# Block sums of turned activations: from VectorE to a GpSimd sequence of their own, with one turning step placed later

## The chip, the cores and the metric

The kernel runs on one core of one Trainium2 chip. The metric is the device time in microseconds (us), lower is better. A core has TensorE (PE in the profile, with its weight loads as PEld), VectorE (DVE), ScalarE (ACT), GpSimd (POOL) and SyncE (SP, which here issues all DMA transfers). Each runs its own instruction stream in order, and waits on semaphores for the others.

## What is computed

Per batch of 8, with 1024 rows of width 1024, in float32:

```
x = x + attention(layernorm(x), ctx, mask)       # 64 memory rows per batch, one head
x = x + base + experts, on h = layernorm(x):
    base    = h @ weight.T                        # 1024 x 1024
    experts = 2.0 * sum over the top 2 of 8 experts of  w_e * (h @ A_e.T) @ B_e.T     # rank 16
```

The dense product `base` takes most of TensorE's time.

## The kernel before, in words

The 8192 rows are 64 tiles of 128 rows; two tiles make a pair (32 pairs), and from pair 2 on four pairs in flight make one turn of the loop `quad(u)` (L973), which finishes the pairs u and v = u+1 and prepares n = u+2, m = u+3 and f = u+4. There are 15 quads, u = 2, 4, ... 30; `first()` (L792) does pairs 0 and 1 and the start-up.

**The dense product is done with block sums** (a Strassen-like scheme). A pair's turned activations form a 2 x 2 grid of blocks: `has[u][:, r]` and `hbs[u][:, r]` are the two halves of the contraction for tile r. `block_sums` (L557) makes four sums of the four blocks, in two steps:

```
s1 = a21 + a22 ; s2 = s1 - a11      # one()
s4 = a12 - s2  ; s3 = a11 - a21     # two()
```

`rt_sums_steps` (L571) calls it for a pair (the pair sums, 128 x 512 each; the names in the profile are `s`), and `joint_sums` (L678) for the two pairs of a quad together (the joint sums, same size; `s_j` and `q_j`). The sums of the weights (`weight_sums`, `quarter_sums`) are made once, in the start-up and the first quad. All of these run on VectorE, by `tt` (`nc.vector.tensor_tensor`). `product(u, i)` (L638) multiplies with the pair sums: product 1 uses `has` itself, 6 uses s2, 7 uses s3; their blocks of 8 matmuls of 128 x 512 are `ch` in the profile.

**The joint products** (`joint`, L692) are where pairs u and v are multiplied together, one quarter of the output columns and rows at a time: joint 5, 3, 2 and 4 in this order at the end of each quad. Each is eight blocks of four (or so) matmuls of 128 x 256. Two PSUM banks are cut into four half banks p2, p5 (names `ju`), p4 and chain (`jl`). What matters here is that p5 and chain are used more than once within a joint product:

```
        block(p5, s1, q1, True)
        part(v, 1, p5)        
        block(chain, s2, q2, False)
        part(u, 1, chain)
        hook(5)
        block(p5, s4, b22, False)
        block(chain, s3, q3, False)
```

(some lines between them are left out; `part` is VectorE's add of a half bank into x, L714). So the block with s4 can start only when VectorE's add of p5 is done. `hook(step)` runs the functions given for that place: it is the way in which work of other stages is written into a joint product.

**Order.** `tc.manual_schedule` (L1125) keeps each listed engine's instructions in the order in which the program writes them; the order is thus written out by hand in `quad`. The lines that matter in a quad: `rt_turn(v)` (L985), pair sums of v (L1017 to L1021), joint sums for joint products 5 and 3 (L1046, L1057), `rt_turn(n)` in hook 5 of joint 3 (L1079), joint sums for 2 and 4 (L1089 to L1091, the second step in hook 2 of joint 2), pair sums of n in hook 5 of joint 4 (L1113).

**Turning.** `rt_turn` (L498) turns the two tiles of a pair: `rt_turn_tile` (L491) issues two VectorE block transposes (STREAM_TRANSPOSE, 128 x 512) from the tile `hs` (loaded by SyncE into `ring`, a pool of 6 buffers) to `has` and `hbs`.

**Buffers.** The pool `sums` has one buffer each for the tags s2, s3, q3 and q4, and two for s14. Pair sums s2 and s3 share the first two with the first and second of the joint sums, so a new sum can be written only after TensorE has read the last one.

Of the kernel before, what the change touches and what calls it, by code (L numbers as in the profile page):

```python
# [14 lines left out]
ALU = mybir.AluOpType  # L15
# [9 lines left out]
def kernel(  # L25
# [10 lines left out]
    nc = tc.nc  # L36
# [37 lines left out]
    mm, tt = nc.tensor.matmul, nc.vector.tensor_tensor  # L74
# [12 lines left out]
    def transpose_blocked(dst, src):  # L87

        nc.vector.transpose(  # L89
            dst.rearrange("p k (t i) -> p t k i", i=NB),  # L90
            src.rearrange("p t (k i) -> p t k i", i=NB),
        )
# [121 lines left out]
    def x_stats(u: int):  # L214
        x_sums(u)
        x_squares(u)
        x_root(u)
# [46 lines left out]
    def f_rows(u: int, fetch: bool = True):  # L264

        nm, std = fts.pop(u)
        rstd = small.tile([P, 2, 1], F32, tag="rstdf", name=f"rstdf_{u}")
        nc.vector.reciprocal(rstd, std)
        nmr = small.tile([P, 2, 1], F32, tag="nmrf", name=f"nmrf_{u}")
        tt(nmr, nm, rstd, ALU.mult)  # L270
        for r in range(2):
            h = ring.tile([P, D], F32, tag="ring", name=f"h_{u}_{r}")
            hss.setdefault(u, []).append(h)
            nc.scalar.activation(  # L274
                h, xts[u][r], AF.Identity, bias=nmr[:, r, :], scale=rstd[:, r, :]
            )
        norm_send(u, fetch)
# [100 lines left out]
    def att_sc(u: int):  # L378
        sc = ps_at.tile([P, 2, M], F32, tag="at", name=f"sc_{u}")
        nc.tensor.transpose(sc.rearrange("p j m -> p (j m)"), scs.pop(u), ident)  # L380
        scs[u] = sc
# [82 lines left out]
    def norm_send(u: int, fetch: bool = True):  # L464

        hds[u] = dram.tile([2 * P, D], F32, tag="hd", name=f"hd_{u}")
        hs_in, hss[u] = hss[u], []
        for r in range(2):
            nc.sync.dma_start(out=hds[u][r * P : (r + 1) * P, :], in_=hs_in[r])
        if fetch:  # L470
            norm_fetch(u)
# [10 lines left out]
    def h_tiles(u: int):  # L482
        has[u] = turned.tile([P, 2, KH, P], F32, tag="hA", name=f"hA_{u}")
        hbs[u] = turned.tile([P, 2, KH, P], F32, tag="hB", name=f"hB_{u}", bufs=3)
# [6 lines left out]
    def rt_turn_tile(u: int, r: int):  # L491
        if r == 0:
            h_tiles(u)
        half = KH * NB
        for t, c in ((has[u], 0), (hbs[u], half)):
            transpose_blocked(t[:, r], hss[u][r][:, :, c : c + half])

    def rt_turn(u: int):  # L498
        for r in range(2):
            rt_turn_tile(u, r)  # L500
# [56 lines left out]
    def block_sums(outs, a11, a12, a21, a22):  # L557

        s1, s2, s3, s4 = outs

        def one():
            tt(s1, a21, a22, ALU.add)
            tt(s2, s1, a11, ALU.subtract)

        def two():
            tt(s4, a12, s2, ALU.subtract)
            tt(s3, a11, a21, ALU.subtract)

        return one, two

# [67 lines left out]
    def product(u: int, i: int, between=None, after: int = 0):  # L638

        if i == 1:  # L640
            pps[u] = bank_of(f"b5_{u}") if u < 2 else None, bank_of(f"ch_{u}")
        b5, chain = pps[u]
        if i == 1:
            block(chain, has[u][:, 0], w11, True, between, after)
        elif i == 5:
            block(b5, sms[u][:, 0], t1, True, between, after)
        elif i == 6:
            block(chain, sss[u][1], t2, False, between, after)
        elif i == 7:
            block(chain, sss[u][2], t3, False, between, after)  # L650
        else:
            lora(u, chain, 1, HB, HB)
# [320 lines left out]
    def quad(u: int):  # L973

        v, n, m, f = [u + i for i in range(1, 5)]
        more = n < NP
        far = f < NP
        b = f // PPB
        new_mem = far and f % PPB == 0

        product(u, 1, (lambda: att_sc(n)) if u == 2 else None, 1)
        pending.pop()()
        product_add(u, 1)
        rt_low_rank_tile(u, 0)
        rt_turn(v)  # L985
        product(u, 6)
        if more:
            x_stats(m)
        if u == 2:
            att_divide(n)  # L990
            att_turn_p(n)
        if more:
            att_turn(m)
        product_add(u, 6)
        if u == 2:
            quarter_sums("t4", t4)
        if new_mem:
            mask_bias(b)
            send_mem(b)
        if far:  # L1000
            load_xs(f)
            load_xt(f)
        rt_low_rank_tile(u, 1)
        product(u, 7)
        rt_top(u)
        product_add(u, 7)
        if more:
            att_readout(n)
            att_scores(m)
            rt_turn_low_rank(u)  # L1010
            att_add(n)

        if more:
            product(v, 1, {0: lambda: att_sc(m), 2: lambda: product(u, 8)})
            att_rstd(m)
            att_exp(m)
            one, two = rt_sums_steps(v)  # L1017
            one()
            product_add(u, 8)
            product_add(v, 1)  # L1020
            two()  # L1021
            f_sums(n)
            att_divide(m)
            rt_low_rank_tile(v, 0)
            product(v, 6, lambda: att_turn_p(m), 1)
            f_squares(n)
        else:
            rt_sums(v)
            product(v, 1, {0: lambda: rt_turn_low_rank(u), 2: lambda: product(u, 8)})
            product_add(u, 8)  # L1030
            product_add(v, 1)
            rt_low_rank_tile(v, 0)
            product(v, 6)
        if far:
            att_turn(f)
        product_add(v, 6)
        rt_low_rank_tile(v, 1)
        product(v, 7)
        if new_mem:
            turn_mem(b)  # L1040
        rt_top(v)
        if more:
            f_std(n)
            f_rows(n)
        product_add(v, 7)
        one, two = joint_sums(5, u)  # L1046
        one()
        if more:
            att_readout(m)
        if far:  # L1050
            att_scores(f)
        if u == 2:
            quarter_sums("w21", w21)
        if more:
            rt_turn_low_rank(v)
            att_add(m)
        two()  # L1057

        def low_v():
            product(v, 8)  # L1060
            product_add(v, 8)

        if more:
            hooks = {2: [low_v]}
        else:
            hooks = {1: [lambda: rt_turn_low_rank(v)], 3: [low_v]}
        if new_mem:
            void_mem(b)
        if far:
            x_sums(f)  # L1070
            x_squares(f)
            x_root(f)
            hooks[3] = [lambda: att_sc(f)]
        end_5 = joint(5, u, hooks)

        hooks = {1: [end_5]}
        if more:
            f_sums(m)
            hooks[5] = [lambda: rt_turn(n)]  # L1079
        if far:  # L1080
            hooks[2] = [lambda: att_rstd(f), lambda: att_exp(f)]
            hooks[7] = [lambda: att_divide(f)]
        end_3 = joint(3, u, hooks)
        if m + 2 < NP:
            load_xs(m + 2)
            if (f + 2) % PPB == 0 and f + 2 < NP:
                load_mem((f + 2) // PPB)

        one, two = joint_sums(2, u)  # L1089
        one()  # L1090
        hooks = {1: [end_3], 2: [two]}  # L1091
        if more:
            f_squares(m)
            f_std(m)
            hooks[1].append(lambda: f_rows(m, False))
        if far:
            hooks[3] = [lambda: att_turn_p(f)]
        end_2 = joint(2, u, hooks)

        def rows_0():  # L1100
            end_2()
            for p in (u, v):
                store(p, 0)
                if not more:
                    store(p, 1, ts(1, HB))
            if more:
                norm_fetch(m)
            if m + 2 < NP:
                load_xt(m + 2)

        hooks = {1: [rows_0]}
        if more:
            hooks[5] = [lambda: rt_sums(n)]  # L1113
        end_4 = joint(4, u, hooks, not more)

        def last():
            end_4()
            if more:
                for p in (u, v):
                    store(p, 1)  # L1120

        pending.append(last)

    engines = mybir.EngineType
    with tc.manual_schedule(engines={engines.PE, engines.DVE, engines.Activation, engines.SP}):  # L1125
        first()
        for q in range(1, NQ):
            quad(2 * q)
        pending.pop()()
# [43 lines left out]
```

## Time and profile before

| | us |
|---|---|
| median of 3 runs (1132.64 to 1134.44) | 1132.66 |
| the profiled execution, whole | 1133.88 |
| its span, first to last instruction | 1132.1 |
| one quad (from 382.38 to 451.20) | 68.82 |
| of it busy: TensorE / VectorE / ScalarE / GpSimd | 68.46 / 51.07 / 34.89 / 0 |
| one block sum on VectorE, 128 x 512 | 0.69 |

The profile is that of one execution. Busy times count instructions that compute; a line such as `L714 DVE TENSOR_TENSOR xt<-ju,xt 128x256` names the line of the kernel, the engine, the operation, and output <- inputs by the program's names with the numbers left out. In a timeline, a line gives the start, the time from the first start to the last end, how many such instructions follow one another, and in brackets idle time of the engine in front of it with what ended it. Matmuls are pipelined and their ends modelled: the distance between the starts of two blocks tells more than the duration of one.

### The profile page before, as it was taken

The numbers are of one execution on the slowest core, as the hardware profiler recorded it, in microseconds if no ns is written. First come the engines' busy times: TensorE is split into PE (matmuls) and PEld (weight loads), VectorE is DVE, ScalarE is ACT, GpSimd is POOL, SyncE is SP. The second block draws the span as 40 slices with busy tenths as digits, with TensorE's granted clock in tenths as the row PEclk, the third lists the DMA queues.
The fourth block names the chain that finished last, engine by engine and source line by source line (L and its number), as shares of the span: only waits on it lengthen the run. The fifth ranks groups of instructions, "written<-read, shape, count | busy, mean of one in ns | idle before, by whom it ended". The sixth has DMA issues, their size and how long they took to land.

```text
span 1132.1 us, 15632 instructions
## 1 busy us (share of the span) xinstructions
PE 1117.1 (99%) x5490; PEld 771.2 (68%) x5490; DVE 850.1 (75%) x2099; ACT 553.8 (49%) x1047; POOL 1.0 (0%) x16
## 2 busy tenths in 40 slices
PE   8999999999999999999999999999999999999998
PEld 5555576775867768676685766758677686766767
DVE  6679887777688677886778767787777877867665
ACT  4576563735537354472635736356373544635010
POOL 0000000000000000000000000000000000000000
PEclk9999999999999999999999999999999999999999
DMA  9966256552664726537263474534645554352401
GB/s 215 234 196 196 75 168 194 161 201 97 173 191 120 234 94 174 169 113 260 89 201 120 150 223 130 186 122 155 189 131 186 153 158 155 112 186 75 150 0 75
DMA packets 104462, 175.73 MB, mean 155 GB/s; under 512 B 11904, under 2 KB 76544, under 8 KB 104384
## 3 DMA queue, kind: packets, MB, share of 16 engines
q1 hardware_dynamic: 104384, 174.73, 50.6%
q8 instruction: 43, 0.70, 0.3%
q14 instruction: 35, 0.29, 0.1%
HBM read 107.84 MB, written 66.85 MB: 154 GB/s over the span
## 4 chain that ended last, share of the span: by engine, by line
PE 81%; DVE 11%; DMA 6%; SPq 1%; issue 1%; DVEq 0%
PE ch L631 28%; PE jl L631 12%; PE pa L513 10%; PE ju L631 9%; PE ro L420 5%; PE sct L367 5%; DVE xt L714 3%; PE ju L623 2%; PE ch L623 2%; PE jl L623 2%; DMA mem<-in_ctx_dram 2%; PE plain L631 2%; DVE hA L89 2%; DVE hB L89 1%; DMA xs<-in_x_dram 1%; SPq L83 1%
## 5 line engine op out<-in xcount | busy, mean ns | idle before, releaser
L631 PE MATMUL ch<-t,s 128*128 128x512 f32 x496 | 224.6, 592 | 0.0
L714 DVE TENSOR_TENSOR xt<-jl,xt 128x256 f32<-128x256 f32 (+1 forms) x301 | 139.2, 484 | 112.7 <-PE jl L631 72.5
L193 ACT ACTIVATE junk<-xt 128x1024 bf16<-128x1024 f32 x60 | 63.3, 1055 | 199.7 <-DMA xt<-in_x_dram 198.3
L631 PEld LDWEIGHTS ch<-t,s 128*128 128x128 f32 x496 | 88.5, 190 | 86.1 <-issue 86.1
L631 PE MATMUL ch<-w,hA 128*128 128x512 f32 x248 | 115.9, 593 | 0.0
L714 DVE TENSOR_TENSOR xt<-ju,xt 128x256 f32<-128x256 f32 (+1 forms) x150 | 80.1, 551 | 42.4 <-PE ju L631 41.5
L620 DVE TENSOR_TENSOR xt<-ch,xt 128x512 f32<-128x512 f32 x124 | 85.0, 685 | 33.9 <-PE ch L631 24.5
L274 ACT ACTIVATE h<-xt,nmrf,rstdf 128x1024 f32<-128x1024 f32 x60 | 71.2, 1234 | 52.5 <-DVE nmrf L270 52.5
L620 DVE TENSOR_TENSOR xt<-ro,xt 128x512 f32<-128x512 f32 x128 | 80.4, 683 | 6.0 <-PE ro L420 6.0
L513 PEld LDWEIGHTS pa<-art_sb,hA 128*128 128x128 f32 x512 | 68.5, 190 | 23.2 <-issue 18.9
L631 PEld LDWEIGHTS ch<-w,hA 128*128 128x128 f32 x248 | 44.7, 190 | 43.0 <-issue 42.1
L89 DVE STREAM_TRANSPOSE xT<-xs 128x1024 f32<-128x1024 f32 x60 | 70.5, 1213 | 0.7 <-DMA xs<-in_x_dram 0.7
L513 PE MATMUL pa<-art_sb,hA 128*128 128x136 f32 x512 | 69.9, 279 | 0.0
L202 ACT ACTIVATE junk<-xt,nm 128x1024 bf16<-128x1024 f32 x60 | 68.9, 1148 | 1.9
L513 PE MATMUL pa<-art_sb,hB 128*128 128x136 f32 x512 | 69.7, 279 | 0.0
L253 ACT ACTIVATE junk<-xt,nmf 128x1024 bf16<-128x1024 f32 x60 | 68.7, 1146 | 1.1
L367 PEld LDWEIGHTS sct<-xT,memT_True 128*64 128x64 f32 x960 | 51.8, 137 | 22.7 <-issue 16.7
L513 PEld LDWEIGHTS pa<-art_sb,hB 128*128 128x128 f32 x512 | 64.1, 190 | 0.0
L420 PE MATMUL ro<-mem,pt 64*128 64x512 f32 x256 | 63.6, 615 | 0.4 <-ACT pt L411 0.4
L243 ACT ACTIVATE junk<-xt 128x1024 bf16<-128x1024 f32 x60 | 62.9, 1049 | 1.6 <-DVE xt L620 0.6
L367 PE MATMUL sct<-xT,memT_True 128*64 128x128 f32 x960 | 59.0, 276 | 0.0
L372 ACT COPY scts<-sct 128x128 f32<-128x128 f32 x32 | 8.5, 266 | 102.5 <-PE sct L367 102.5
(183 smaller groups left out, 1852.1 us busy)
## 6 DMA issues: line engine op xcount, KB each, us to landing
xt<-in_x_dram SPq DMA_DIRECT2D x64, 512.0 KB, 6.2
out_dram<-xt SPq DMA_DIRECT2D x62, 512.0 KB, 3.7
xs<-in_x_dram SPq DMA_DIRECT2D x240, 128.0 KB, 3.8
hd<-h SPq DMA_DIRECT2D x60, 512.0 KB, 2.7
hs<-hd SPq DMA_DIRECT2D x240, 128.0 KB, 3.3
mem<-in_ctx_dram SPq DMA_DIRECT2D x16, 256.0 KB, 5.5
w<-in_w_t_dram SPq DMA_DIRECT2D x16, 256.0 KB, 11.5
md<-memc_False SPq DMA_DIRECT2D x7, 256.0 KB, 2.9
```

What stands on the lines that cost most here:

```text
L89: nc.vector.transpose(dst.rearrange("p k (t i) -> p t k i", i=NB), src.rearrange("p t (k i) -> p t k i", i=NB),)
L193: nc.scalar.activation(nowhere, xts[u][r], AF.Identity, accum_out=sm[:, r, :])
L202: nc.scalar.activation(nowhere, xts[u][r], AF.Square, bias=stds[u][:, r, :], accum_out=ss[:, r, :],)
L253: nc.scalar.activation(nowhere, xts[u][r], AF.Square, bias=nm[:, r, :], accum_out=ss[:, r, :])
L274: nc.scalar.activation(h, xts[u][r], AF.Identity, bias=nmr[:, r, :], scale=rstd[:, r, :])
L367: mm(sct[r * M : (r + 1) * M, :], mt[:, k, :], x_ts[u][r][:, k, :], start=(k == 0), stop=(k == KD - 1),)
L420: mm(ro, pts[u][rows, :], m[rows, ts(c, HB)], start=True, stop=True)
L513: mm(pa[:, r, :], h, art_sb[:, k, :], start=(k == 0), stop=(k == KD - 1))
L620: tt(xc, bank, xc, ALU.add)
L623: mm(bank, axwts[u][:, r, :], lb_sb[:, c0 : c0 + n], start=alone, stop=True, skip_group_check=True)
L631: mm(bank, a[:, k, :], w[:, k, :], start=(start and k == 0), stop=(k == n - 1), skip_group_check=True)
L714: tt(xc, src, xc, ALU.add)
```

## The change

The four operations of `block_sums` are issued on GpSimd instead of VectorE, for pair sums and joint sums alike, in the start-up too. GpSimd is added to the engines whose order is that of the program, so its sums form one sequence in the written order. In `quad`, the turning of pair n is divided: tile 0 stays in hook 5 of joint 3, tile 1 goes to hook 5 of joint 2.

```diff
         s1, s2, s3, s4 = outs
 
+        by = nc.gpsimd.tensor_tensor
+
         def one():
-            tt(s1, a21, a22, ALU.add)
-            tt(s2, s1, a11, ALU.subtract)
+            by(s1, a21, a22, ALU.add)
+            by(s2, s1, a11, ALU.subtract)
 
         def two():
-            tt(s4, a12, s2, ALU.subtract)
-            tt(s3, a11, a21, ALU.subtract)
+            by(s4, a12, s2, ALU.subtract)
+            by(s3, a11, a21, ALU.subtract)
...
             f_sums(m)
-            hooks[5] = [lambda: rt_turn(n)]
+            hooks[5] = [lambda: rt_turn_tile(n, 0)]
...
             hooks[1].append(lambda: f_rows(m, False))
+            hooks[5] = [lambda: rt_turn_tile(n, 1)]
...
-    with tc.manual_schedule(engines={engines.PE, engines.DVE, engines.Activation, engines.SP}):
+    with tc.manual_schedule(engines={engines.PE, engines.DVE, engines.Activation, engines.SP, engines.Pool}):
```

## The prediction

> **What bounds the kernel now.** I read the page's busy times first, then the windows of several repetitions of the loop over groups of four pairs (a "quad", 15 of them), then TensorE's waits, then the timelines of TensorE and VectorE inside one quad.
>
> ```profile
> PE 1117.1 (99%) x5490; PEld 771.2 (68%) x5490; DVE 850.1 (75%) x2099; ACT 553.8 (49%) x1047; POOL 1.0 (0%) x16
> ```
>
> ```profile
> 313.56:382.38 68.82, 68.46 (x341) 48.01 (x341) 53.89 (x135) 35.93 (x67) 0.00 (x0) 1.00 0.51 160
> 382.38:451.20 68.82, 68.46 (x342) 48.02 (x341) 51.07 (x127) 34.89 (x66) 0.00 (x0) 1.00 0.53 162
> ```
>
> Columns of the second view: length of the window, then busy time (and instructions) of PE, PEld, DVE, ACT, POOL, then granted clock, DMA share, GB/s. A quad takes 68.82 us and TensorE is busy in all but 0.36 of it, at full clock. A matmul's recorded end is modelled, so I look at starts: a block of four 128x256 matmuls follows the last one after 0.86 us nearly everywhere, and one place breaks the pitch.
>
> ```profile
> 430.83 1.03 PE L631 MATMUL ju<-w,s_j 128*128 128x256 f32 x4
> 431.70 1.03 PE L631 MATMUL jl<-w,s_j 128*128 128x256 f32 x4
> 432.56 1.03 PE L631 MATMUL ju<-w,q_j 128*128 128x256 f32 x4
> ...
> 438.75 1.03 PE L631 MATMUL ju<-w,s_j 128*128 128x256 f32 x4
> 439.62 1.03 PE L631 MATMUL jl<-w,s_j 128*128 128x256 f32 x4
> 441.01 1.13 PE L631 MATMUL ju<-w,q_j 128*128 128x256 f32 x4 [0.36 <-DVE xt L714]
> ```
>
> These are the same three steps (s1 into p5, s2 into the chain, s4 into p5 again) of joint 3 (430.83) and of joint 2 (438.75). Joint 3 keeps the pitch. In joint 2 the third step should start at 439.62+0.86 = 440.48 and starts at 441.01: 0.53 us late. The reason is on VectorE, which must empty p5 before TensorE may write it again:
>
> ```profile
> 431.90 0.42 DVE L714 TENSOR_TENSOR xt<-ju,xt 128x256 f32<-128x256 f32 x1
> ...
> 439.33 0.68 DVE L566 TENSOR_TENSOR q_j<-hB,s_j 128x512 f32<-128x512 f32 x1
> 439.93 0.69 DVE L567 TENSOR_TENSOR q_j<-hB,hB 128x512 f32<-128x512 f32 x1
> 440.53 0.42 DVE L714 TENSOR_TENSOR xt<-ju,xt 128x256 f32<-128x256 f32 x1
> ```
>
> In joint 3 that add starts 0.20 after its block's pitch ends (431.70 to 431.90). In joint 2 it could start at 439.8, but stands behind two block sums and starts at 440.53. The view of TensorE's waits has this as the only one of size:
>
> ```profile
> PE ju L631 <- DVE xt L714: 4.7, 13, 0.4
> ```
>
> Thirteen times, once in each quad up to the one at 933 us. The kernel is bound by TensorE's instruction stream; VectorE costs time only there.
>
> **What the change can gain.** 13 x 0.53 = 6.9 us. In the quad at 1002 us the same step is 0.24 late (1058.17 where 1057.93 is due): +0.2. In the first quad, joint 5 starts its s2 step at 149.00 where 148.54 is due and its s4 step at 150.26 where 149.86 is due, with block sums at 147.00 to 148.20 in front of the adds on VectorE. Other quads lose 0.15 in joint 5 (425.55 for 425.40), where two adds stand between the steps and no sum does; that stays. So the first quad has 0.46+0.40-0.15 = 0.7 to give. Sum: 6.9+0.2+0.7 = 7.8 us. More cannot come of it: the rest of the stream stands at its pitch, apart from 15 x 0.15 = 2.2 us in joint 5.
>
> **What is taken from VectorE.** 124 instructions of the pair sums and 120 of the joint sums:
>
> ```profile
> L563 DVE TENSOR_TENSOR s<-s,hA 128x512 f32<-128x512 f32 x31 | 21.4, 691 | 1.1
> L566 DVE TENSOR_TENSOR s<-hB,s 128x512 f32<-128x512 f32 x31 | 21.3, 687 | 0.6
> L567 DVE TENSOR_TENSOR s<-hA 128x512 f32<-128x512 f32 x31 | 21.2, 684 | 0.0
> L562 DVE TENSOR_TENSOR s<-hA,hB 128x512 f32<-128x512 f32 x31 | 21.1, 681 | 0.0
> ```
>
> Each is 0.69 us, 244 x 0.687 = 168 us, 11.0 us of each quad's 51. All but the places above lie under TensorE's stream, so 160 of them give nothing.
>
> **What GpSimd pays.** No such operation runs there before. The nearest row:
>
> ```profile
> masks.py:199 POOL TENSOR_SCALAR_AFFINE_SELECT ident<-ident 128x128 f32<-128x128 f32 x1 | 0.3, 292 | 0.0
> L157 POOL MEMSET eps_sb<- 128x1 f32 x1 | 0.1, 99 | 0.0
> ```
>
> From it a one-input operation costs 0.10 us and (292-100)/128 = 1.5 ns an element: 0.87 us for 512 elements, a lower bound; twice the slope for two inputs gives 1.64, an upper bound. Here a rule speaks against the change: the Trainium skill, GPSIMD Engine Reference, Engine selection, gives elementwise adds to VectorE, because GpSimd takes about twice as long (4497 ns for 2048 elements; by the same page's 2.6 cycles an element at 1.2 GHz an estimate of 1.17 us for 512). If the sums lay on the path, 244 x (1.17-0.69) = 117 us would be lost. I take 1.2 us, between the two bounds, and ask where each result is first read. The sums' buffers are single, so a sum also starts only when TensorE has read the former content.
>
> Pair sums of v: the turned tiles are there at 389.97, the two buffers are free at 391.4 and 396.75, TensorE reads s2 at 407.10 and s3 at 412.50. Over 10 us spare.
> Joint 5: the second sum's buffer is free when the product block before it ends, 416.0. Three operations remain: 417.3, 418.5, 419.7. First reads: 424.54 (s2), 425.55 (s4), 426.51 (s3). Spare 7.
> Joint 2: the first buffer comes free with joint 3's s1 step, about 431.8. Four in a row end at 433.0, 434.2, 435.4, 436.6; reads, with the wait gone, at 438.75, 439.62, 440.48, 441.78. Spare 5.
> Pair sums of n: three in a row from 448.1, done at 451.7; reads 456.76 (387.94+68.82) and later. Spare 6.
>
> The tightest is joint 2's fourth: it decides at (441.78-431.8)/4 = 2.5 us an operation, half again the upper bound. While a sum waits for a buffer, only other sums queue behind it on GpSimd; no DMA is issued there. TensorE's wait for VectorE becomes one for GpSimd. So this costs nothing, and its cover is 5 us of joint 3's and joint 2's stream.
>
> **The moved turning.** Tile 1's two STREAM_TRANSPOSE (0.67 each, 1.34 us a quad) go from before joint 3's last adds to joint 2, behind the chain's s2 add, at about 441.1 to 442.4. The add of p5 stands ahead of them; the next adds are due at 442.8 and 443.5, so they fit into what was a 2.19 us idle gap of VectorE before 443.47. GpSimd's pair sums of n can then start at 442.4 rather than 435.6, but s2's buffer holds them until 448.1 anyway. The tile's input is freed 7 us later; SyncE's next loads into that ring are at 446.35. Nothing on SyncE is moved. Cost 0, below nothing excluded, because no transpose precedes a late step in the timeline; if the cover failed, at most 15 x 1.34 = 20 us.
>
> **Contention.** The Trainium skill, SBUF — State Buffer, Who interferes with whom, says that a VectorE operation with two SBUF inputs and a GpSimd operation that reads SBUF exclude each other for a whole instruction, and that one with at most one SBUF input does not. No row here shows them side by side. The adds that TensorE waits for read a PSUM bank and SBUF (xt<-ju,xt), so by the rule they are free. The two-SBUF operations left are small ones (routing, softmax, 0.16 to 0.29 us), mostly outside GpSimd's four windows, and their readers on TensorE come 2 to 3.7 us later (routing of u ends 396.87, read at 400.56). In the start-up the weight and quarter sums are also of that kind: four batches at 55 to 60, 100 to 108, 116 to 119 and 141 to 144 us, about 14 GpSimd operations beside them, 14 x (1.2-0.69) = 7 us of delay for VectorE in four portions of about 2, under slacks of 2.9 to 3.7 (xT ends 68.05, read 71.78). I put it at 0.3 us, bounds 0 and 5.
>
> **The sum.** The profiled execution: 1133.88 with a span of 1132.1, so 1.8 lie outside the span. 1132.1-7.8+0.3 = 1124.6 span, 1126.4 execution. It stands 1.2 above the median of 1132.66; from the median 1132.66-7.5 = 1125.2.
>
> **Rivals.**
> Adds held by GpSimd (slower). The first joint 2 sum is released by the matmul that also releases joint 3's p5 add (431.90); the pair sum of n likewise beside joint 4's p5 add (448.22). That add ends at 432.32 for a need at 432.56, slack 0.24. If the lock covers PSUM-and-SBUF adds too and GpSimd wins, the add is held 1.2 and TensorE loses 1.0, twice a quad: 15 x 2.0 = 30-7.5: 1155. It decides from a hold of 0.24+0.53/2 = 0.5 us on. For it: the two starts coincide by construction; against: the rule. 0.14.
> GpSimd too slow (slower). At 3.5 us an operation joint 2's fourth sum is 4 us late in 15 quads: 1185. Against: both bounds. 0.05.
> Part of the gain spent in start-up or in small holds elsewhere: 1127 to 1130. 0.13.
> The wait stays, another instruction of VectorE standing ahead of p5's add (a held small one): within 2 us of 1132.7. 0.06.
> All waits named go: 1125.2. 0.62.
>
> **How the numbers follow.** About 0.2% (2.3 us) can be told from no change. Faster 0.62+0.13 = 0.75 (0.74 with the smallest partial gains left to the next case), same 0.07, slower 0.19. The range takes in the first case, the partial gain and the unchanged one: 1123 (the 7.8 and a little of joint 5) to 1136 (a hold just past its deciding point); outside lie most of the two slower cases, under 0.2.
>
> **What would show it.** A quad of 68.3 us; the s4 step of joint 2 at pitch, TensorE's wait for VectorE's add gone; POOL some 26% busy (244 x 1.2 = 293 us), VectorE near 680. Wrong if L714's adds of 128x256 last over 0.42 or start late after their block when POOL is busy, if TensorE waits for POOL, or if a GpSimd sum lasts over 2.5 us.

## The result and the profile after

| | before | after |
|---|---|---|
| median, us | 1133.01 (4 runs) | 1124.83 (4 runs, 1124.73 to 1125.48) |
| ratio to before | | 0.9928, 95% interval 0.9913 to 0.9942 |
| the profiled execution / its span | 1133.88 / 1132.1 | 1124.92 / 1123.1 |
| one quad, start to start of product 1 | 68.82 | 68.22 |

The change takes 0.7% off, and 1125.2 had been forecast. In the changed file the lines from L560 on stand two lower (L631 is now L633, L623 is L625, L714 is L716, L620 is L622, the four sums are L564, L565, L568, L569).

The first line of the page: VectorE is down from 850 to 743 us of busy time, GpSimd up from 1 to 312.

```profile
PE 1113.6 (99%) x5490; PEld 774.0 (69%) x5490; DVE 743.1 (66%) x1855; ACT 553.4 (49%) x1047; POOL 312.4 (28%) x260
```

The window of one quad (length; busy PE, PEld, DVE, ACT, POOL; clock, DMA share, GB/s): 0.60 us shorter, with TensorE idle for 0.08 of it rather than 0.36.

```profile
379.12:447.34 68.22, 68.14 (x342) 48.16 (x340) 43.37 (x110) 34.77 (x66) 20.38 (x17) 1.00 0.53 162
```

TensorE's timeline at joint product 2, the place that was 0.53 late: the block with s4 now follows at the pitch, 437.41 after 436.55.

```profile
435.68 1.03 PE L633 MATMUL ju<-w,s_j 128*128 128x256 f32 x4
436.55 1.03 PE L633 MATMUL jl<-w,s_j 128*128 128x256 f32 x4
437.41 1.03 PE L633 MATMUL ju<-w,q_j 128*128 128x256 f32 x4
```

VectorE's timeline beside it: the add of p5 starts 0.20 after its block's pitch ends, and VectorE stood idle for 1.29 us ahead of it, where it had been working through two sums.

```profile
436.75 0.42 DVE L716 TENSOR_TENSOR xt<-ju,xt 128x256 f32<-128x256 f32 x1 [1.29 <-PE ju L633]
```

Of the waits of TensorE for these adds, 4.7 us in 13 places before, this is left, both in joint 5 of the first quad:

```profile
PE jl L633 <- DVE xt L716: 0.4, 1, 0.4
...
PE ju L633 <- DVE xt L716: 0.2, 1, 0.2
```

GpSimd's timeline at the tightest place, the four joint sums for joint products 2 and 4. They are there at 430.2, 431.5, 432.9 and 434.1, and TensorE first reads them at 435.68, 436.55, 437.41 and 438.70: 4.6 us of cover for the last.

```profile
428.91 1.27 POOL L564 TENSOR_TENSOR s_j<-hB 128x512 f32<-128x512 f32 x1 [11.89 <-PE ju L633]
430.26 1.28 POOL L565 TENSOR_TENSOR s_j<-s_j,hB 128x512 f32<-128x512 f32 x1
431.61 1.27 POOL L568 TENSOR_TENSOR q_j<-hB,s_j 128x512 f32<-128x512 f32 x1
432.84 1.27 POOL L569 TENSOR_TENSOR q_j<-hB,hB 128x512 f32<-128x512 f32 x1
```

**Where the 9.0 us of span come from.** I lined up the starts of TensorE's blocks in the two timelines. The start-up gives 0.92 (the first loads landed earlier, and a transpose at 33 us waited less). I don't count it to the change: over the kernels of this study, with one profile each, the first block of the first quad starts at 105.0 to 106.3 us, with no order by what they do (106.33 before, 105.41 after, 105.26 in one that leaves the whole start-up as it was). The first quad gives 0.36, twelve quads 0.605 each, the next to last 0.49, and the last loses 0.06: 0.92+0.36+7.26+0.49-0.06 = 8.97.

Within one of the twelve quads, against before: joint 5 is 0.07 longer, 0.04 come back at the start of joint 2, and the late step of joint 2 gives 0.63, which is 0.53 of lateness and 0.10 by which the block after a stall had been longer (0.96 rather than 0.86 from its start to the next).

### The profile page after: what moved, and what is told of

Same layout as the page of the kernel before. It is cut to its first block, busy times and chain, and to the rows that moved or that the text cites. A ratio compares the mean times of both kernels' runs of the same rounds, so it can differ in the third digit from the quotient of the medians.

```text
span 1123.1 us, 15874 instructions
## 1 busy us (share of the span) xinstructions
PE 1113.6 (99%) x5490; PEld 774.0 (69%) x5490; DVE 743.1 (66%) x1855; ACT 553.4 (49%) x1047; POOL 312.4 (28%) x260
## 4 chain that ended last, share of the span: by engine, by line
PE 98%; DVE 1%; DMA 0%; ACT 0%; issue 0%; SPq 0%; DVEq 0%; ACTq 0%
PE ch L633 28%; PE jl L633 18%; PE ju L633 14%; PE pa L513 11%; PE ro L420 5%; PE sct L367 5%; PE ju L625 3%; PE jl L625 3%; PE plain L633 3%; PE ch L625 2%; PE trw L553 1%; PE j L633 1%; DMA xt<-in_x_dram 0%; PE ptp L409 0%; PE tr_x L342 0%; DVE xt L622 0%
## 5 line engine op out<-in xcount | busy, mean ns | idle before, releaser
L716 DVE TENSOR_TENSOR xt<-jl,xt 128x256 f32<-128x256 f32 (+1 forms) x301 | 140.0, 486 | 164.5 <-PE jl L633 111.2
L633 PE MATMUL ch<-t,s 128*128 128x512 f32 x496 | 224.7, 592 | 0.0
L193 ACT ACTIVATE junk<-xt 128x1024 bf16<-128x1024 f32 x60 | 63.3, 1055 | 206.3 <-DMA xt<-in_x_dram 205.3
L633 PEld LDWEIGHTS ch<-t,s 128*128 128x128 f32 x496 | 88.5, 190 | 86.2 <-issue 86.1
L622 DVE TENSOR_TENSOR xt<-ch,xt 128x512 f32<-128x512 f32 x124 | 85.0, 685 | 58.8 <-PE ch L633 34.6
L716 DVE TENSOR_TENSOR xt<-ju,xt 128x256 f32<-128x256 f32 (+1 forms) x150 | 80.3, 552 | 63.5 <-PE ju L633 62.6
L633 PE MATMUL ch<-w,hA 128*128 128x512 f32 x248 | 115.9, 593 | 0.0
L564 POOL TENSOR_TENSOR s<-hA,hB 128x512 f32<-128x512 f32 x31 | 39.6, 1278 | 266.0 <-DVE hB L89 201.6
L622 DVE TENSOR_TENSOR xt<-ro,xt 128x512 f32<-128x512 f32 x128 | 81.3, 683 | 11.9 <-PE ro L420 11.9
L633 PEld LDWEIGHTS ch<-w,hA 128*128 128x128 f32 x248 | 44.7, 190 | 43.0 <-issue 42.1
L564 POOL TENSOR_TENSOR s_j<-s 128x512 f32<-128x512 f32 x15 | 19.1, 1275 | 187.4 <-PE ch L633 187.4
L564 POOL TENSOR_TENSOR s_j<-hB 128x512 f32<-128x512 f32 x15 | 19.0, 1268 | 172.5 <-PE ju L633 172.5
```

The source lines that it names most:

```text
L564: by(s1, a21, a22, ALU.add)
L622: tt(xc, bank, xc, ALU.add)
L633: mm(bank, a[:, k, :], w[:, k, :], start=(start and k == 0), stop=(k == n - 1), skip_group_check=True)
L716: tt(xc, src, xc, ALU.add)
```

## Was it the sums or the moved turning?

The two edits work on the same wait. My prediction gave the whole gain to the sums and nothing to the turning. Two kernels do one part each.

**The sums alone** (against the changed kernel):

```diff
-            hooks[5] = [lambda: rt_turn_tile(n, 0)]
+            hooks[5] = [lambda: rt_turn(n)]
...
-            hooks[5] = [lambda: rt_turn_tile(n, 1)]
```

> The sums on GpSimd, the turning of both tiles left in joint product 3. Theory A (the add of p5 in joint 2 was late by 0.73 us because VectorE had a backlog; whatever takes more than that from ahead of it removes the whole wait): the sums alone take 1.4 us directly ahead of the add, so the time is that of the changed kernel, 1124.8 to 1125.2, a quad 68.2. Rival B (the moved turning is needed too, since with it left in place the transposes and a held softmax multiplication still push the add back): between 1126 and 1129, a quad 68.3 to 68.6.

Measured: 1125.56, ratio to before 0.9931 (0.9918 to 0.9945); a quad 68.25. That lies between the two forecasts and close to A: the whole gain but 0.04 us a quad comes without the moved turning. The 0.04 are lost at the start of joint 2 (the second of its blocks starts 0.04 late there, as it did before).

**The turning alone** (against the kernel before, sums on VectorE):

```diff
-            hooks[5] = [lambda: rt_turn(n)]
+            hooks[5] = [lambda: rt_turn_tile(n, 0)]
...
+            hooks[5] = [lambda: rt_turn_tile(n, 1)]
```

> Only the turning of tile 1 moved to joint product 2, all sums on VectorE as before. Theory A: 1.34 us of transposes go from ahead of the p5 add to behind it, more than the 0.73 us of backlog, so nearly the whole gain comes without GpSimd: a quad 68.15 to 68.3, and 1124.5 to 1126. The prediction as written (moving the turning gains nothing, only the sums on VectorE stand in the way): 1132 to 1133, a quad 68.82. Besides: if the 0.07 us a quad that joint 5 lost in the changed kernel comes from TensorE waiting for two engines at the block with s4, it is not lost here (1.01 us from the s2 block's start to the s4 block's, against 1.10).

Measured: 1125.34, ratio 0.9927 (0.9914 to 0.9941); a quad 68.28. Two lines without GpSimd give the gain of the whole change but for 0.06 us a quad. So the prediction's step on the turning falls. VectorE's timeline of this kernel in joint products 3 and 2:

```profile
432.49 0.42 DVE L714 TENSOR_TENSOR xt<-jl,xt 128x256 f32<-128x256 f32 x1 [0.52 <-PE jl L631]
...
436.36 0.68 DVE L566 TENSOR_TENSOR q_j<-hB,s_j 128x512 f32<-128x512 f32 x1
436.96 0.68 DVE L567 TENSOR_TENSOR q_j<-hB,hB 128x512 f32<-128x512 f32 x1
437.56 0.41 DVE L714 TENSOR_TENSOR xt<-ju,xt 128x256 f32<-128x256 f32 x1
```

The two sums still stand right in front of the add of p5. But the whole queue is earlier: the s1 block starts at 436.29 here, and the add of p5 comes 1.27 us after that, against 1.78 before (438.75 to 440.53) and 1.07 in the changed kernel. That is just in time: TensorE's s4 block starts 0.02 late and is 0.10 longer.

```profile
436.29 1.03 PE L631 MATMUL ju<-w,s_j 128*128 128x256 f32 x4
437.15 1.03 PE L631 MATMUL jl<-w,s_j 128*128 128x256 f32 x4
438.03 1.13 PE L631 MATMUL ju<-w,q_j 128*128 128x256 f32 x4
```

In the kernel before, VectorE had not one idle line from 432.76, in joint 3, to the end of that add and its neighbour at 441.3. The start of that run:

```profile
432.76 0.43 DVE L714 TENSOR_TENSOR xt<-jl,xt 128x256 f32<-128x256 f32 x1 [0.44 <-PE jl L631]
433.10 0.70 DVE L89 STREAM_TRANSPOSE hA<-hs 128x512 f32<-128x512 f32 x1
...
435.51 0.39 DVE L714 TENSOR_TENSOR xt<-jl,xt 128x256 f32<-128x256 f32 x1
```

In such a stretch everything stands ahead of the late instruction, the transposes 5 to 7 us earlier as much as the sums next to it. I had read only its neighbours.

**Half of the turning alone**: one of tile 1's two transposes moved.

```diff
+    def rt_turn_late(u: int):
+        half = KH * NB
+        transpose_blocked(hbs[u][:, 1], hss[u][1][:, :, half : 2 * half])
...
+            hooks[5] = [lambda: rt_turn_late(n)]
```

> Sums on VectorE; only one of tile 1's two transposes (0.67 us instead of 1.34) goes to joint product 2. Theory A (a backlog of 0.73 us ahead of p5's add, of which TensorE feels 0.53): the add starts 0.67 earlier, at the offset of 0.06 from the earliest it could, ends 0.2 before its block is due, and the whole gain is there: a quad 68.25 to 68.35, 1125.2 to 1126.5. If the gain goes with the amount of VectorE work moved: half of it, a quad 68.55, 1129.

Measured: 1125.71, ratio 0.9938 (0.9925 to 0.9952); a quad 68.27. Half the work moved gives the whole gain, so it doesn't go by the amount. The timeline shows why. VectorE's unbroken run up to the add of p5 goes back to the last add of joint 3, which reads what TensorE has just finished. With the whole turning moved it is the line of 432.49 above: VectorE waited 0.52 for TensorE, and starts 3.80 us ahead of the s1 block. With half of it moved it starts without a wait and yet 3.79 ahead of the s1 block (435.44). In this kernel L714 has become L722:

```profile
431.65 0.42 DVE L722 TENSOR_TENSOR xt<-jl,xt 128x256 f32<-128x256 f32 x1
```

Before, it started at 435.51, 3.24 ahead. So the transposes made it 0.56 late; 0.67 us taken away is already more than TensorE's own progress allows to use. Less than 0.56 was not tried.

## How much cover do the sums have on GpSimd?

**Each sum issued twice, and three times** (same operands, same result):

```diff
-        by = nc.gpsimd.tensor_tensor
+        def by(*args):
+            for _ in range(2):
+                nc.gpsimd.tensor_tensor(*args)
```

> Every sum on GpSimd issued twice in a row, same result: about 2.5 us a sum. By the slack account the fourth sum of joint 2 decides at 2.5 us: with the first starting 0.1 us after joint 3's s1 block is read, it ends about 0.3 us after its block is due, so 0.2 to 0.5 us a quad is lost, 3 to 7 us in all: 1128 to 1132, TensorE waiting for POOL at joint 2's last step only. If the sums had no such cover (TensorE waits wherever they run): 244 x 1.27 = 310 us more. If there is more cover than worked out: 1124.8.

Measured: 1171.64, ratio 1.0339 (1.0323 to 1.0355): a miss, 40 us above what I expected. 10.7 us of it are lost by the end of the first quad (185.13 against 174.47). Of these, 4.1 are two waits of TensorE for VectorE's adds of `ch` and `ro`, which stand behind eight weight sums that GpSimd holds to 1.2 to 1.75 us each. Later quads lose 1.4 to 2.8. The two largest waits of TensorE (lines behind `block_sums` stand two further down again, and L563 is now every sum):

```profile
PE trw L553 <- DVE axl L547: 19.2, 14, 3.5
PE jl L635 <- POOL q_j L563: 12.2, 16, 1.4
```

The second line is the one foretold: joint 2's fourth sum, in 15 of its 16 places. In the quad from 397 us on, its block starts at 457.87 where 457.0 was due, 0.87 late rather than 0.3, because a doubled sum takes 2.62 and each that depends on the one before starts 0.08 later. The first line I had not foretold. It is the routing, small operations on VectorE whose result TensorE transposes. VectorE's timeline there, in the kernel with doubled sums:

```profile
410.29 1.03 DVE L532 CAST idf<-idx 128x4 f32<-128x4 uint32 x1
411.36 1.34 DVE L536 TENSOR_TENSOR we<-iota_e,idf 128x16 f32<-128x16 f32 x2
412.62 0.15 DVE L538 TENSOR_SCALAR w<-e 128x2 f32<-128x2 f32 x1
...
413.01 0.91 DVE L541 TENSOR_TENSOR w<-w,e 128x2 f32<-128x2 f32 x1
...
414.16 1.13 DVE L544 TENSOR_TENSOR we<-we,we 128x16 f32<-128x16 f32 x1
```

Operations that take 0.16 to 0.18 us each elsewhere last until the GpSimd operation beside them is over. One hold costs about 1 us, but in this quad five links of the chain are held (the fifth, L526 at 408.97, stands ahead of the lines shown), as GpSimd is busy all along. From its first operation (L524) to its last (L547) the chain takes 7.1 us, against 3.0 in the kernel before: the 3.7 us of slack that the prediction gave the routing are gone, although no single hold is long. TensorE waits 0.55 us here, and up to 3.5 in other quads.

> Every sum on GpSimd issued three times, about 3.75 us a sum. By the slack account joint 2's third sum ends 2.7 us late and the fourth another 2.4, joint 5's fourth about 0.8: 5 to 6.5 us a quad, 15 quads, 1200 to 1225. The adds that read a PSUM bank and SBUF (L716, 128x256) stay at 0.42 us although GpSimd is then busy for two thirds of the time; under the rival of the prediction (the lock covers them too) many of them last 1 us and more.

Measured in one run: 1359.33, another miss on the same side. TensorE waits 49.0+45.6 us for the joint sums `q_j` and 48.6 for the routing. Quads take 78 to 85 us, and the granted clock is 0.947 over the run, where it was 0.995 to 1.00 in the others, so this time isn't read as slack alone. Its other question has a clear answer. The adds that read a PSUM bank and SBUF, with GpSimd busy 61 of 85 us:

```profile
L718 DVE TENSOR_TENSOR xt<-ju,xt 128x256 f32<-128x256 f32 x75 | 30.5, 423 | 56.9 <-PE ju L635 56.9
```

423 ns on average, as before (422). The changed kernel shows the same at the place that the prediction named: joint 3's add of p5 (428.87) and the first joint sum (428.91) start 0.04 us apart, and the add takes 0.43. The prediction's main rival, that GpSimd holds these adds, is out.

## What was left: joint product 5

Both edits leave joint 5 late, where VectorE's two adds of p5 (0.76 us) stand between two blocks only 0.86 apart. Before, the s4 block starts 1.01 after the s2 block and the next block 0.96 after it (424.54, 425.55, 426.51); in the changed kernel 1.10 and 0.94 (421.44, 422.54, 423.48).

**A block put between the two uses of p5.**

```diff
-        block(p2, a[:, HK:], b21, True)
-        low(u, p2, 0)
+        if r is not None:
+            block(p2, a[:, HK:], b21, True)
+            low(u, p2, 0)
         hook(3)
         block(p5, s1, q1, True)
         part(v, 1, p5)
+        if r is None:
+            block(p2, a[:, HK:], b21, True)
```

In this order, in which a block begun afresh in p2 lies between the two that p5 is to sum, in one bank, joint product 5 no longer comes out right; by what step stays open. The amount of work is the same, and only the time is read.

> The changed kernel, and in joint product 5 the block into p2 goes behind the s1 block into p5 instead of ahead of it, so that two blocks lie between the two uses of p5 and VectorE's two adds (0.76 us) have 1.7 us. The changed kernel loses 0.31 us a quad there (the s4 block starts 1.10 after the s2 block and lasts 0.94, where 0.86 and 0.86 are due). If VectorE's two adds are the cause, all of it goes: a quad 67.9, 15 x 0.31 = 4.6 us less than the changed kernel, 1120.2. If the 0.07 of it that came with GpSimd is TensorE's handling of a second wait whether or not it has to wait, 0.05 to 0.1 a quad stays: 1121.3. If the cause lies elsewhere: 1124.8.

> No GpSimd: only the turning of tile 1 moved, and the same new order in joint product 5. The kernel with the moved turning alone loses 0.24 us a quad in joint 5 and 0.11 in joint 2. Without the first: 15 x 0.24 = 3.6 us less than 1125.3, so 1121.7, a quad 68.04. Moving 168 us of sums to GpSimd would then be worth 0.11 - 0.0 to 0.07 us a quad, 1 to 2 us.

Measured: 1143.61 (1.0093, 1.0078 to 1.0109) and 1145.58 (1.0111, 1.0095 to 1.0126), both slower than before and outside every forecast. TensorE's timeline of the first:

```profile
427.24 1.03 PE L633 MATMUL ju<-w,s_j 128*128 128x256 f32 x4
429.11 1.13 PE L633 MATMUL ju<-w,s 128*128 128x256 f32 x4 [0.85 <-DVE xt L716]
430.08 1.03 PE L633 MATMUL jl<-t,s_j 128*128 128x256 f32 x4
```

The p2 block, meant to fill the time, waits for the adds of p5 itself (they end at 429.05). No add reads p2 there; p2 and p5 are halves of one bank, one tile `ju` in the program, so the program's wait must be for the tile as a whole. In the old order nothing was written to it between the two uses.

**A block of another bank put there**: product 8 of v, moved from ahead of the p2 block to hook 5.

```diff
-            hooks = {2: [low_v]}
+            hooks = {5: [low_v]}
```

> The changed kernel, with product 8 of v (two matmuls of 128x512, 0.86 us) moved in joint product 5 from ahead of the p2 block to between the s2 block and the s4 block: more than the 0.24 us by which VectorE's two adds of p5 are late there, and no block of the same PSUM bank stands between the two uses of p5 (such a block had to wait for the adds too and cost 1.0 us a quad). If the adds were the whole cause, the 0.31 us a quad go: 67.9 a quad, 15 x 0.31 = 4.6 us less than the changed kernel, 1120.2. If TensorE's second wait (for GpSimd) costs 0.07 even when it is met: 1121.3. If the add of product 8 (0.69 us on VectorE) now comes too late for joint product 3's bank: 1124 to 1127.

Measured: 1121.88, ratio 0.9901 (0.9886 to 0.9916). TensorE is busy for the whole quad:

```profile
378.21:446.12 67.91, 67.91 (x342) 48.33 (x341) 43.10 (x110) 34.77 (x66) 20.28 (x17) 1.00 0.53 163
```

The quad is the 67.90 expected, so the lateness of the adds was the whole cause. The total is 1.7 us above the 1120.2 worked out: the first quad, whose weight sums keep VectorE late, takes 69.51 where the changed kernel takes 69.06, and the profiled execution (1121.03) lies 0.85 under the median. It is faster than both kernels: its slowest run took 1123.11, the fastest of the changed kernel 1124.73.

> No GpSimd: the moved turning alone, with product 8 of v moved in the same way. The moved turning alone takes 68.28 a quad, of which 0.24 in joint 5 and 0.11 in joint 2 are TensorE's lateness. Without the first: 68.04 a quad, 15 x 0.24 = 3.6 us less, 1121.5 to 1122. If the sums on VectorE (11 us a quad) are late in front of the moved add: 1123 to 1126, and then the sums on GpSimd are worth something after all.

Measured: 1123.73, ratio 0.9916 (0.9903 to 0.9930), a quad 68.02: the quad of the first forecast, the total of the second. The same edit without GpSimd gets within 0.12 us a quad of it, and the 0.12 are the restart of joint 2's s4 block (0.11 late or long). The next to last quad loses 0.89: there TensorE waits 0.62 us in joint 5 (the block at 1031.71) for adds that stand behind two sums on VectorE (1029.71 and 1030.31). The first quad gives 0.18 back. 12 x 0.12 + 0.89 - 0.18 = 2.1 us: that is what moving 168 us of sums to GpSimd is worth here, by one profile each. The medians lie 1.85 apart, and the intervals of the two ratios overlap.

## The prediction, point by point

**The bound and the place**: right. TensorE's stream bounded the kernel and the one wait that mattered is gone. **The size of the gain**: 7.8 foretold for the span; without the start-up's 0.92, 8.05 measured. Several terms are off and nearly cancel, so that the sum came out this close is in part luck. A late step costs 0.63 rather than 0.53, since the block after a stall is 0.10 longer; 13 x 0.10 = 1.3 us more. The next to last quad gives 0.49 instead of 0.2. The 0.07 lost in joint 5, less the 0.04 won at the start of joint 2, take 0.4 off over twelve quads. And the first quad gives 0.36 where I had 0.7 beside its 0.53: joint 5 there did not gain but lost 0.20, and 0.11 more went at 116 to 120 us. VectorE's timeline in the changed kernel shows the weight sums of that quad held by GpSimd, 1.3 to 1.75 us where each took 0.69, and the adds behind them as late as before (s2 block 0.61 late, 0.46 before).

```profile
139.94 1.32 DVE L613 TENSOR_TENSOR w<-w 128x512 f32<-128x512 f32 x1
141.29 1.65 DVE L614 TENSOR_TENSOR w<-w,w 128x512 f32<-128x512 f32 x1
142.86 1.75 DVE L615 TENSOR_TENSOR w<-w 128x512 f32<-128x512 f32 x1
144.54 0.68 DVE L616 TENSOR_TENSOR w<-w,w 128x512 f32<-128x512 f32 x1
```

So the held sums took the 0.7 and another 0.3 with it: the contention of the start-up was mis-sized (0.3 taken for all of it, bounds 0 and 5).

**GpSimd's price**: 1.2 us taken between 0.87 and 1.64, 1.27 to 1.31 measured. The prediction's estimate of 1.17 from the Trainium skill, GPSIMD Engine Reference, Performance versus the Vector engine, is 8% under it. **The cover**: 5 us for the tightest sum foretold, 4.6 found; from which price it decides, the doubled sums show to be a little under the 2.5 worked out (at 2.62 the fourth is 0.87 late), but the routing decides there as well, whose holds I had not added up along the chain. **Contention**: the Trainium skill, SBUF — State Buffer, Who interferes with whom, agrees with the trace in what the prediction needed of it: adds that read PSUM and SBUF stay at 0.42, operations with two SBUF inputs are held. The page excepts the two-port modes from its second half, and the prediction left that out: some operations with one SBUF input are held too (last section). The softmax's multiplication in the changed kernel, against 292 ns before, is held in 13 of its 32 places, where the prediction had put it mostly outside GpSimd's windows:

```profile
L404 DVE TENSOR_TENSOR s<-s,rden 128x128 f32<-128x128 f32 x32 | 21.7, 677 | 1.1
```

**VectorE's busy time**: near 680 us foretold, 743 measured, a sign that failed. About 40 of the 63 us are operations held by GpSimd, by the groups of VectorE's lines before and after: 12 at the softmax's multiplication, 10 at the routing (L532, L547), 9 at the weight sums, 5 at L170. Much of the rest must be that a sum takes less off the busy time than its 0.69, since an independent instruction behind it starts 0.60 after it (439.33 to 439.93 before). In TensorE's waits none of the 40 shows outside the first quad.

**The step that failed**: "The moved turning ... Cost 0, below nothing excluded, because no transpose precedes a late step in the timeline." The turning alone brings 0.54 us a quad, nearly as much as the sums alone (0.57), and both together 0.60. Transposes did precede the late step, in the same unbroken run of VectorE. The time came out right because either part removes the one wait; the reason given for it was half of the truth.

**The small loss in joint 5** (0.07 a quad) appears in both kernels with GpSimd sums (1.10 from s2 to s4 block) and in neither without (1.01). The block with s4 needs both VectorE's add and GpSimd's sum there. The trace has 159 semaphore instructions of 51 ns ahead of TensorE's weight loads on L633, against 8 on that line before. That these cause the 0.07 is argued, not shown: with the adds no longer late (1121.88) the loss is gone as well, which would fit a second wait that costs only where the first has just been met.

## What to carry to other kernels

When an engine off the path makes the bounding one wait at one place, look back along its timeline to its last idle gap: everything in that run is a candidate, and the cheapest to move is worth as much as the largest, if it takes at least as long as the run is late (0.67 us moved against 0.56 here). Work out the gain from the late starts on the bounding engine, never from the busy time taken off the other: here 168 us moved and 8 were gained, and the two lines that move the turning gave nearly the same alone. The slower engine cost nothing where its results had cover (4.6 us at the tightest), but what its operations hold on a neighbour must be counted link by link along each chain of small operations.

## What the runs showed of the hardware

- Consecutive GpSimd sums of 128x512 start 1.22 us apart, 1.35 if the second reads the first's result. One lasts 1.27; beside VectorE's weight sums, which have two SBUF inputs, 1.6 to 1.7.
- GpSimd also holds VectorE operations with one SBUF input: a TENSOR_SCALAR of 128x64 (L170) took 1.06 us in the median of 8 where it had taken 0.20, and the CAST of 128x4 (L532) up to 0.98 for 0.17, each ending with the GpSimd sum beside it. The page cited on contention lists both as forms that can take the shared ports, when their operands meet the conditions of the two-port modes.
- After a stall TensorE's next block of four 128x256 matmuls is 0.10 us longer than the others, 0.96 for 0.86 from start to start, also where it started only 0.02 us late. Why was not tested.
